# Two dense layers and the bus attention of the second level joined into one stage of a single-core network kernel

## The chip, the cores and the metric

The kernel runs on one core of one Trainium2 chip. It computes a whole four-level network in one launch. The metric is device time in microseconds (us), the median of the runs shown; lower is better. All arithmetic is in f32.

The engines are named as the profile names them: PE (TensorE, matrix multiplies, with PEld for its weight loads), DVE (VectorE), ACT (ScalarE), POOL (GpSimd) and SP (the queue that issues transfers). Each takes its own instructions in order; semaphores join them.

## The reference

The stream `x` has 4 batches of 512 tokens with 128 features (the reference sees the same numbers as 2 x 256 or 4 x 256 in other stages). Every block adds its result to `x` after a layer norm. The change touches three consecutive blocks of the second level:

```python
x = x + _L1_ffn_ref(_layernorm(x), W1, b1, W2, b2)
x = x + _L1_attn_b_ref(_layernorm(x), ...)
x = x + _L1_ffn_ref(_layernorm(x), W1, b1, W2, b2)
```

The dense block is two products with ternary weights and a rectifier between them:

```python
h = relu(einsum('bsd,fd->bsf', x, Wq1) + b1)      # 128 -> 512
out = einsum('bsf,df->bsd', h, Wq2) + b2          # 512 -> 128
```

The bus attention, cut to what matters:

```python
xn = _rms(x, w_norm_in)
route_in = xn.mean(axis=1)
probs = softmax(silu(route_in @ router_w1) @ router_w2 + router_b2)
ssm_out = scan(state = lam * state + (1 - lam) * xn)          # per channel, over tokens
a1, a2 = softmax(q1 k1 * sc), softmax(q2 k2 * sc)             # two heads of 32
slr_out = ((a1 - slr_lam * a2) @ v) @ slr_wo
mixed = ssm_out + (p_medium + p_full) * slr_out               # last token also gets arc_ctx
out = concat([mixed, xn]) @ mix_w
out = residual + _rms(out, w_norm_out)
summary = out.mean(axis=1) @ bus_compress
published = summary @ bus_publish
out = out + 0.1 * (published @ bus_expand)    # the softmax is over one key and is 1
```

## The kernel before

`x` stays on chip as `self.x`, 128 tokens on the partitions and 16 chunks of 128 features beside each other, four chunks to a batch. `moments` (lines 369 to 375) takes mean and variance of each chunk after every change of `x`, `normed` (377 to 393) makes the normalised copy `xn`, and `transposed` (360) turns four chunks into `xT`, with features on the partitions.

The program is a list of stages, `STAGES` (2881). One stage follows the other; the list has `"L1a", "L1f", "L1b", "L1f"`, so the dense layer `L1f` (1444) runs once before and once after the bus attention `L1b` (1486). Each stage opens its own pools for on-chip memory and for the eight banks of the matmul accumulator (PSUM), and closes them at its end.

`L1f` runs over the four batches. Per batch it multiplies four blocks of 128 x 128 by 512 columns (`ps_h`), ACT rectifies each (line 1459), 16 products of 128 x 128 x 128 sum into `ps_o` (1463), and DVE adds `ps_o` to `x` (`add_to_x`, 440) and takes moments. POOL adds the bias (`bias_x`, 434). Two banks hold `ps_h` and the transposes, two hold `ps_o`.

`L1b` is a pipeline of 16 scores, four per batch (`score`, 1578). A score is two products on 32 rows each into `ps_s` (two banks); DVE takes the row maxima (1586), ACT two exponentials with sums (1589), DVE the reciprocals (1593, 1594), POOL scales one half (1595), and DVE joins both into `a` (1598), which frees the banks. Three scores may be in flight (six banks); the last two banks serve everything else. `turn_scores` (1602) transposes `a` three slots later (`LAG`). A `Plan` (261) calls the other functions at slots written out by hand (1734 to 1751): the other batches' `turn`, `project` and `values`, the routers, and, for batch b, `context`, `mix` and `out` at slots 4b+7 to 4b+9. `finish` (1650) closes two batches at a time, batches 0 and 1 at slot 14, batches 2 and 3 after the loop: the root of the mean square on ACT (which needs another function table than the exponential), eight scalings on DVE, two additions per batch on POOL, and the mean over tokens on PE. Then two products by bus matrices are made for all four batches (1767), and each batch gets the result added and its moments taken (1772 to 1781).

The order of the work: everything called with `pin=True` or through `keep_in_program_order` stays in the order written; PE's matmuls in `L1b` are all pinned, as are the exponentials, and POOL's scalings there. Other DVE and ACT instructions are ordered by the framework's scheduler. At its start `L1b` calls `roots(0, B - 1)`, which waits for the moments of three batches, and then `turn(0)`. `net.there` (2905) tells the second `L1f` that only one batch is normalised at first. `L2a` (1784), the stage behind, calls `norm` (413), which normalises three batches unless the stage before it did so (`self.ahead`).

Of the kernel before, what the change touches and what calls it, by code (L numbers as in the profile page):

```python
# [11 lines left out]
F32 = mybir.dt.float32  # L12
# [262 lines left out]
class Net:  # L275
# [1168 lines left out]
    def L1f(self):  # L1444
        nc, tc = self.nc, self.tc
        w1, w2 = self.W("f1_w1"), self.W("f1_w2")
        with (
            tc.tile_pool(name="l1f_s", bufs=1) as sp,
            tc.tile_pool(name="l1f_r", bufs=2) as rp,
            tc.tile_pool(name="l1f_p", bufs=2, space=PSUM) as pp,  # L1450
        ):
            xT, rest = self.norm(pp, self.there)
            for b in range(B):
                self.bias_x(b, "f1_b2")
                h = rp.tile([P, 4, S], F32, name="h")
                for m in range(4):
                    ps = pp.tile([P, S], F32, tag="mm", name="ps_h")
                    self.mm(ps, w1[:, m * P : m * P + P], xT[:, b * S : b * S + S])
                    nc.scalar.activation(h[:, m], ps, AF.Relu, bias=self.W("f1_b1")[:, m : m + 1])
                po = pp.tile([P, CB, D], F32, tag="o", name="ps_o")  # L1460
                for j in range(CB):
                    for m in range(4):
                        self.mm(
                            po[:, j],
                            h[:, m, j * P : j * P + P],
                            w2[:, m * D : m * D + D],
                            start=m == 0,
                            stop=m == 3,
                        )
                self.add_to_x(b, po)  # L1470
                if b == 0:
                    rest()

# [12 lines left out]
    def L1b(self):  # L1486
# [5 lines left out]
        SC, EPS, LAG = 32.0**-0.5, 1.1920929e-07, 3  # L1492
        with (
            tc.tile_pool(name="l1b_s", bufs=1) as sp,
            tc.tile_pool(name="l1b_r", bufs=2) as rp,
            tc.tile_pool(name="l1b_p", bufs=1, space=PSUM) as pp,
        ):

            def bank(name, shape, tag="mm", bufs=2):
                return pp.tile(shape, F32, tag=tag, name=name, bufs=bufs)  # L1500

            mv = self.mv
            rs = sp.tile([P, 2, NC], F32, name="rs")
            tiny = sp.tile([P, 1], F32, name="tiny")
            nc.gpsimd.memset(tiny, EPS * 1e-5)
            x0 = sp.tile([P, NC, D], F32, name="x0")
            xh, xT = self.xn, self.xT

            def roots(b0, b1):
                cs = slice(CB * b0, CB * b1)
                var = mv[:, cs, 1]
                nc.scalar.activation(rs[:, 0, cs], var, AF.Sqrt, bias=tiny, scale=1.0 + EPS)
                nc.scalar.activation(rs[:, 1, cs], var, AF.Sqrt, bias=self.eps["1e-5"])
                nc.vector.reciprocal(rs[:, :, cs], rs[:, :, cs])


            def centred(out, b, k, eng):
                for c in range(CB * b, CB * b + CB):  # L1520
                    i = eng.tensor_scalar(
                        out[:, c],
                        self.x[:, c],
                        mv[:, c, 0:1],
                        rs[:, k, c : c + 1],
                        ALU.subtract,
                        ALU.mult,
                    )
                    if eng is nc.gpsimd:
                        tc.keep_in_program_order(i)  # L1530
# [3 lines left out]
            def turn(b):  # L1534
                centred(xh, b, 0, nc.vector)
                ps = bank("ps_tr", [P, CB, P])
                for j in range(CB):
                    self.tr(ps[:, j], xh[:, CB * b + j])
                i = nc.scalar.activation(
                    xT[:, b * S : b * S + S],  # L1540
                    ps.rearrange("p j t -> p (j t)"),
                    AF.Identity,
                    scale=self.W("b1_wni"),
                    accum_out=route[:, b : b + 1],
                )
                tc.keep_in_program_order(i)
# [4 lines left out]
            q, k, v, ema, a, aT, cT, mixed, y, t = ({} for _ in range(10))  # L1551

            def project(b):
                bs = slice(b * S, b * S + S)
                ps = bank("ps_q", [64, S])
# [3 lines left out]
                ps = bank("ps_k", [64, S])  # L1559
# [4 lines left out]
            def values(b):  # L1564
                ps = bank("ps_v", [P, CB, 32])
                for j in range(CB):
# [5 lines left out]
                i = nc.gpsimd.tensor_scalar(  # L1572
                    ema[b], xT[:, b * S : b * S + S], one_l, None, ALU.mult
                )
                tc.keep_in_program_order(i)
                nc.vector.tensor_tensor_scan(ema[b], lam, ema[b], 0.0, ALU.mult, ALU.add)

            def score(n):
                b, j = divmod(n, CB)
                ps = bank("ps_s", [P, 2, S], "sc", 3)  # L1580
                for h in range(2):
                    r = slice(32 * h, 32 * h + 32)
                    self.mm(ps[:, h], q[b][r, j * P : j * P + P], k[b][r, :], pin=True)
# [4 lines left out]
                for h, to in ((1, e), (0, ps[:, 0])):  # L1588
                    i = nc.scalar.activation(
                        to, ps[:, h], AF.Exp, bias=m[:, h : h + 1], accum_out=z[:, h : h + 1]  # L1590
# [1340 lines left out]
```

## Time and profile before

| what | value |
|---|---|
| median of 3 runs | 2410.75 us (2405.64 to 2413.52) |
| the profiled execution | 2416.43 us, span 2414.7 us |
| instructions | 33640 |
| PE busy in the span | 2156.9 us (89%), mean granted clock 0.928 |
| DVE, ACT, POOL busy | 1724.6 (71%), 1291.2 (53%), 610.4 us (25%) |
| first `L1f`: first transpose to last product | 1142.5 to 1176.0 us |
| `L1b`: to the first score, to the last score | 1184.6 us, 1270.1 us |
| second `L1f`: first `ps_h` to last product | 1310.7 to 1345.3 us |
| `L2a`: first product | 1354.4 us |

The span is what lies between the first and last instruction of the profiled execution; 1.7 us lie around it. All times inside it are counted from its start. "Granted clock" is the share of PE's full speed that the throttle let through in a window. A busy PE is not PE at its peak: at half clock the same product counts twice the busy time. The three stages that the change joins take 202.8 us here, 8.4% of the span.

### The profile page before, as it was taken

How to read it: one execution, taken by the hardware profiler on the slowest of the kernel's cores; microseconds unless marked ns; L12 is line 12 of the kernel's file. 1: busy time of each engine (PE TensorE's matmuls, PEld its weight loads, DVE VectorE, ACT ScalarE, POOL GpSimd, SP SyncE). 2: the span in 40 equal slices, each digit the busy share in tenths (PEclk: the TensorE clock that was granted, in tenths of full speed). 3: DMA queues.
4: the chain of work that ended last, by engine and by line, in shares of the span. 5: the costliest groups of instructions: out<-in, count | busy, mean ns of one | idle time of the engine just before them, and what ended most of it. 6: DMA issues, size and time to landing. Idle time of an engine off the chain costs nothing.

```text
span 2414.7 us, 33640 instructions
## 1 busy us (share of the span) xinstructions
PE 2156.9 (89%) x12151; PEld 1011.0 (42%) x12151; DVE 1724.6 (71%) x3373; ACT 1291.2 (53%) x2558; POOL 610.4 (25%) x441
## 2 busy tenths in 40 slices
PE   7999999999899998999876789889869998888868
PEld 2343334643333334667434446542214666422213
DVE  6666666579998774656464674679997557678995
ACT  4555555279845665342442463666645445476643
POOL 1100010010000001022153410048871015148871
PEclk9999999999899998999867989999989999988988
DMA  3000001400000000400200024245543430044550
GB/s 144 1 1 1 1 1 43 100 1 2 2 1 2 1 1 15 113 16 24 86 1 1 0 57 88 59 122 145 160 140 59 87 49 2 1 122 139 161 152 18
DMA packets 68885, 127.85 MB, mean 53 GB/s; under 512 B 9328, under 2 KB 29296, under 8 KB 68080
## 3 DMA queue, kind: packets, MB, share of 16 engines
q1 hardware_dynamic: 68720, 125.71, 19.8%
q8 instruction: 96, 1.57, 0.3%
q14 instruction: 69, 0.57, 0.1%
HBM read 119.91 MB, written 5.64 MB: 52 GB/s over the span
## 4 chain that ended last, share of the span: by engine, by line
PE 65%; DVE 16%; issue 9%; ACT 6%; DMA 2%; POOL 1%; SPq 0%; POOLq 0%; DVEq 0%; ACTq 0%
PE ps_o L346 14%; PE ps_s L346 9%; PE ps_st L346 6%; PE ps L346 5%; PE ps_c L346 5%; PE ps_g L346 4%; DVE hc L2373 4%; PE ps_x L346 3%; PE ps_u L346 2%; PE ps_v L346 2%; DVE ps_du L2368 2%; DVE e L850 2%; PE ps_tr L351 2%; PE ps_q L346 2%; DMA wt<-dram 2%
## 5 line engine op out<-in xcount | busy, mean ns | idle before, releaser
L2378 POOL TENSOR_TENSOR hc<-hc,cr 128x1024 f32<-128x1024 f32 x126 | 297.6, 2363 | 117.6 <-DVE hc L2373 112.8
L2373 DVE TENSOR_TENSOR_SCAN hc<-da,ps_du 128x1024 f32<-128x1024 f32 x128 | 291.0, 2275 | 0.0
L346 PE MATMUL ps_s<-k,q 32*128 32x512 f32 (+3 forms) x1088 | 254.1, 609 | 8.2 <-DVE mx L850 4.4
L538 ACT ACTIVATE e<-ps_s,mx 128x512 f32<-128x512 f32 x256 | 172.6, 686 | 139.5 <-DVE mx L533 132.9
L346 PE MATMUL ps_du<-du,spread 64*128 64x512 f32 x512 | 164.0, 713 | 64.6 <-DVE hc L2373 64.4
L2354 ACT ACTIVATE da<-da,am 128x512 f32<-128x512 f32 x248 | 165.8, 715 | 62.3 <-DMA da<-dram 57.5
L346 PE MATMUL ps<-xT,w_L2f 128*128 128x512 f32 (+1 forms) x416 | 194.6, 615 | 0.0
L936 DVE TENSOR_REDUCE nm<-ps_s 128x1 f32<-128x512 f32 x256 | 162.5, 683 | 37.7 <-PE ps_s L346 28.8
L1022 ACT ACTIVATE e<-ps_st 128x512 f32<-128x512 f32 x256 | 138.4, 595 | 88.7 <-PE ps_s L346 61.8
L533 DVE TENSOR_REDUCE mx<-ps_s 128x2 f32<-128x1024 f32 x128 | 150.9, 1219 | 43.8 <-PE ps_s L346 43.6
L2368 DVE TENSOR_TENSOR ps_du<-ps_du,br 128x1024 f32<-128x1024 f32 x128 | 154.9, 1211 | 30.3 <-PE ps_du L346 30.2
L861 ACT ACTIVATE e<-e,mx 128x512 f32<-128x512 f32 (+3 forms) x256 | 140.1, 549 | 18.7 <-DVE mx L850 18.4
L346 PE MATMUL ps_st<-q,k 32*128 32x512 f32 x512 | 143.6, 645 | 0.0
L346 PE MATMUL ps_s<-q,k 64*128 64x512 f32 x512 | 129.1, 618 | 2.2 <-ACT e L538 1.7
L346 PE MATMUL ps_c<-e,vz 128*64 128x512 f32 x512 | 123.5, 604 | 0.8 <-POOL vz L549 0.8
L1945 DVE SCALAR_TENSOR_TENSOR t<-ps,w_L2f,t 128x512 f32<-128x512 f32 (+1 forms) x104 | 76.7, 747 | 62.5 <-PE ps L346 41.7
L850 DVE CUSTOM_DVE_ANT_0 e<-ps_s,tri 128x512 f32<-128x512 f32 (+3 forms) x256 | 109.2, 485 | 14.7 <-PE ps_s L346 14.7
L346 PEld LDWEIGHTS ps_du<-du,spread 64*128 64x128 f32 x512 | 45.8, 203 | 173.3 <-issue 118.8
L346 PEld LDWEIGHTS ps_s<-k,q 32*128 32x128 f32 x1088 | 86.5, 196 | 72.8 <-issue 30.6
L346 PEld LDWEIGHTS ps<-xT,w_L2f 128*128 128x128 f32 (+1 forms) x416 | 75.7, 191 | 97.0 <-issue 75.2
L549 POOL TENSOR_TENSOR vz<-v,z 128x512 f32<-128x512 f32 x32 | 33.4, 1043 | 322.8 <-DVE z L547 293.7
L659 DVE TENSOR_TENSOR hc<-hc,wt 128x1024 f32<-128x1024 f32 x80 | 94.7, 1188 | 25.5 <-ACT hc L1948 12.2
(500 smaller groups left out, 4188.7 us busy)
## 6 DMA issues: line engine op xcount, KB each, us to landing
da<-dram SPq DMA_DIRECT2D x124, 256.0 KB
da<-dram SPq DMA_DIRECT2D x124, 255.5 KB
wt<-dram SPq DMA_DIRECT2D x144, 128.0 KB
wt<-dram SPq DMA_DIRECT2D x32, 256.0 KB
dram<-dl SPq DMA_DIRECT2D x16, 256.0 KB
wt<-dram SPq DMA_DIRECT2D x16, 224.0 KB
wt<-dram SPq DMA_DIRECT2D x16, 192.0 KB
wt<-dram SPq DMA_DIRECT2D x16, 160.0 KB
```

The costliest lines, as they stand in the source:

```text
L346: i = self.nc.tensor.matmul(out, lhsT, rhs, start=start, stop=stop)
L533: nc.vector.tensor_reduce(mx, sc, AX.X, ALU.max, negate=True)
L538: nc.scalar.activation(es[n][:, hh], sc[:, hh], AF.Exp, bias=mx[:, hh : hh + 1], accum_out=z[m][:, j, hh : hh + 1],)
L659: nc.vector.tensor_tensor(h, h, wt[b, k][:, r:e], ALU.mult)
L850: red = nc.vector.tensor_tensor_reduce(e[:, i, :w], sc[i][:, :w], tri[:, S - w :], -1.0, BIG, ALU.add, ALU.min, mx[:, i : i + 1],)
L861: nc.scalar.activation(e[:, i, :w], e[:, i, :w], AF.Exp, bias=mx[:, i : i + 1], scale=-1.0, accum_out=z[:, i : i + 1],)
L936: nc.vector.tensor_reduce(nm[:, j, i, 9:10], sc, AX.X, ALU.max, negate=True)
L1022: keep(nc.scalar.activation(es_[n][:, i], sc, AF.Exp))
L2354: nc.scalar.activation(da[n][:, t, t:], src[:, t:], AF.Exp, scale=am[:, at : at + 1])
L2368: keep(nc.vector.tensor_tensor(dx[n], dx[n], br, ALU.mult))
L2373: keep(nc.vector.tensor_tensor_scan(h, a, x, 0.0, ALU.mult, ALU.add))
L2378: keep(nc.gpsimd.tensor_tensor(hc[n], hc[n], cr, ALU.mult))
```

## The change

`L1f` and `L1b` go, and one stage `L1m` stands in their place; `STAGES` becomes `"L1a", "L1m", "L2a"`, and `net.there` goes. What differs inside:

- **One pipeline.** Batches 0 and 1 pass the first dense layer ahead of the loop, batches 2 and 3 in slots 0 to 7 beside the scores of batches 0 and 1. The second dense layer of batch b runs in slots 4b+12 to 4b+15; the loop has 28 slots, 16 of them with a score.
- **Per-batch finish.** `finish` is split into `out` (slot 4b+8), `weighed` (4b+9), `summary` (4b+10) and `normed` (4b+11), each for one batch.
- **Bus matrices multiplied once.** `transfer` (slot 5) makes the product of the three bus matrices by transposes, products and DVE copies. `summary` takes the token mean spread over 128 columns and needs one product per batch.
- **Roots on POOL.** Every inverse root in the stage is now two small POOL instructions, one that scales and adds, one that raises to the power -1/2. ACT's roots and DVE's reciprocals go.
- **Routers in pairs.** `router1` to `router3` and `marks1` to `marks3` run for two batches at a time, twice.
- **Banks.** Two scores in flight instead of three (four banks), three banks for everything else, one bank shared by `ps_o` and `ps_y`; `LAG` is 2 instead of 3.
- **Ahead of L2a.** `normed_ahead` in the last slot normalises batches 0 to 2 for `L2a`.

The core of the diff:

```diff
-    def L1f(self):
...
-    def L1b(self):
+    def L1m(self):
...
-        SC, EPS, LAG = 32.0**-0.5, 1.1920929e-07, 3
+        SC, EPS, LAG = 32.0**-0.5, 1.1920929e-07, 2
...
+            def root(out, in_, scale, eps):
+                keep(nc.gpsimd.tensor_scalar(out, in_, scale, eps, ALU.mult, ALU.add))
+                keep(
+                    nc.gpsimd.tensor_tensor(
+                        out, out, half.to_broadcast(list(out.shape)), ALU.pow
+                    )
+                )
...
+            def normed(b):
+                cs = slice(CB * b, CB * b + CB)
+                root(self.rs[:, cs], mv[:, cs, 1], 1.0, 1e-5)
+                self.centred(b)
+            def turned(b):
+                self.transposed(
+                    pp, "mm", xT[:, b * S : b * S + S], xn[:, CB * b : CB * b + CB], pin=True
+                )
+                self.bias_x(b, "f1_b2")
+                h[b] = rp.tile([P, 4, S], F32, name="h")
+            def hidden(b, m):
+                ps = bank("ps_h")
+                self.mm(ps, w1[:, m * P : m * P + P], xT[:, b * S : b * S + S], pin=True)
+                nc.scalar.activation(h[b][:, m], ps, AF.Relu, bias=self.W("f1_b1")[:, m : m + 1])
+            def dense(b, j):
+                if j == 0:
+                    po[b] = bank("ps_o", (P, CB, D), "o", 1)
+                for m in range(4):
+                    self.mm(
+                        po[b][:, j],
+                        h[b][:, m, j * P : j * P + P],
+                        w2[:, m * D : m * D + D],
+                        start=m == 0,
+                        stop=m == 3,
+                        pin=True,
+                    )
+                if j == CB - 1:
+                    self.add_to_x(b, po[b])
...
+            def residual(b):
+                cs = slice(CB * b, CB * b + CB)
+                root(rs[:, 1, cs], mv[:, cs, 1], 1.0, 1e-5)
+                scaled(x0, b, 1, nc.gpsimd)
...
-                ps = bank("ps_s", [P, 2, S], "sc", 3)
+                ps = bank("ps_s", (P, 2, S), "sc", 2)
...
-            def finish(b0):
...
+            def transfer():
+                w = self.W("b1_bc")
+                for n in ("b1_bp", "b1_be"):
+                    ps = bank("ps_t", (P, P))
+                    self.tr(ps, w)
+                    t = rp.tile([P, P], F32, name="busT")
+                    nc.vector.tensor_copy(t, ps)
+                    ps = bank("ps_w", (P, D))
+                    self.mm(ps, t, self.W(n), pin=True)
+                    w = bus if n == "b1_be" else rp.tile([P, D], F32, name="busw")
+                    nc.vector.tensor_copy(w, ps)
+            def summary(b):
+                ps = bank("ps_mean", (P, P))
+                for j in range(CB):
+                    self.mm(
+                        ps, y[b][:, j], self.ones, start=j == 0, stop=j == CB - 1, pin=True
+                    )
+                ctx = rp.tile([P, P], F32, name="ctx")
+                nc.vector.tensor_scalar(ctx, ps, 0.1 / S, None, ALU.mult)
+                ps = bank("ps_be", (P, D))
+                self.mm(ps, ctx, bus, pin=True)
+                xb = self.x[:, CB * b : CB * b + CB]
+                nc.vector.tensor_tensor(
+                    xb, ps.unsqueeze(1).to_broadcast([P, CB, D]), xb, ALU.add
+                )
+                self.moments(b)
...
+            def layer(b, n):
+                plan.at(n, turned, b)
+                plan.at(n, hidden, b, 0)
+                plan.at(n + 1, hidden, b, 1)
+                plan.at(n + 1, hidden, b, 2)
+                plan.at(n + 2, hidden, b, 3)
+                plan.at(n + 2, dense, b, 0)
+                plan.at(n + 2, dense, b, 1)
+                plan.at(n + 3, dense, b, 2)
+                plan.at(n + 3, dense, b, 3)
+            for b in (2, 3):
+                layer(b, 4 * b - 8)
+            for b in range(1, B):
+                if b > 1:
+                    plan.at(4 * b - 5, first_root, b)
+                plan.at(4 * b - 4, turn, b)
+                plan.at(4 * b - 2, project, b)
+                plan.at(4 * b - 1, values, b)
...
+            plan.at(5, transfer)
             for b in range(B):
...
+                n = 4 * b
+                plan.at(n + 2, residual, b)
+                plan.at(n + 6, context, b)
+                plan.at(n + 7, mix, b)
+                plan.at(n + 8, out, b)
+                plan.at(n + 9, weighed, b)
+                plan.at(n + 10, summary, b)
+                plan.at(n + 11, normed, b)
+                layer(b, n + 12)
+            self.ahead = False
+            self.normed(B - 1, B)
+            for b in range(2):
+                turned(b)
+                for m in range(4):
+                    hidden(b, m)
+            for j in range(CB):
+                dense(0, j)
+            first_root(0)
+            for j in range(CB):
+                dense(1, j)
+            first_root(1)
             turn(0)
...
+            last = 4 * B + 11
+            for n in range(last + 1):
                 if n < NC:
                     score(n)
...
+                if n == last:
+                    self.normed_ahead()
                 plan.run(n)
...
-    "L1a", "L1f", "L1b", "L1f",
+    "L1a", "L1m",
```

## The prediction

> **What bounds the kernel now.** First comes the page with its 40 slices of 60.4 us. The three stages lie at 1142 to 1345 us, slices 18 to 22, and there PE's busy share and PE's granted clock dip together:
>
> ```profile
> PE   7999999999899998999876789889869998888868
> PEclk9999999999899998999867989999989999988988
> ```
>
> Then the busy times by stretch, cut at the stages' borders. The columns are the stretch, its length, the busy time with the instruction count of PE, PEld, DVE, ACT and POOL, PE's clock, and the transfers:
>
> ```profile
> 1142.50:1176.00 33.50, 33.15 (x176) 22.91 (x176) 8.02 (x41) 13.57 (x22) 1.44 (x2) 0.95 0.48 194
> 1176.00:1184.60 8.60, 5.27 (x14) 1.76 (x14) 6.78 (x29) 2.51 (x8) 0.10 (x1) 0.80 0.00 0
> 1184.60:1258.00 73.40, 63.45 (x223) 27.94 (x223) 41.63 (x88) 35.36 (x88) 32.71 (x25) 0.65 0.00 1
> 1258.00:1270.10 12.10, 3.69 (x18) 3.58 (x18) 8.19 (x16) 5.35 (x9) 10.29 (x10) 0.67 0.00 0
> 1270.10:1310.70 40.60, 23.17 (x105) 14.78 (x104) 19.99 (x70) 9.32 (x19) 11.89 (x11) 0.67 0.00 1
> 1310.70:1345.30 34.60, 33.95 (x172) 22.51 (x172) 11.07 (x41) 12.92 (x21) 4.01 (x5) 0.91 0.00 1
> 1345.30:1354.40 9.10, 3.45 (x12) 2.22 (x13) 8.64 (x33) 4.17 (x6) 3.64 (x5) 0.62 0.00 0
> ```
>
> The two dense layers (first and sixth line) are bound by PE at nearly full clock. Between them PE has work for part of the time only, and does it at 0.65 to 0.67 of its speed. The fourth line is `finish(0)` in slot 14, the fifth holds the last score, `finish(2)`, the bus and the norm, the seventh opens L2a. Last, the chain of waits shows what the fifth line's end consists of:
>
> ```profile
> 1287.87 0.50 ACT y L1645
> 1288.39 1.28 ACT L357
> 1289.68 0.31 ACT ms L357
> 1290.02 0.21 DVE ms L358
> 1290.26 4.31 DVE y L1657 x8
> 1294.69 1.27 POOL y L1665
> 1296.01 1.88 PE ps_mean L346 x8
> ...
> 1310.10 0.59 ACT xT L365
> ```
>
> It is one serial walk through ACT, DVE, POOL and PE, in which PE is late with nothing. So the change can gain where PE idles or runs slowly, up to what the PE work itself takes.
>
> **The change, by four pieces.** The whole is 1142.5 to 1354.4, 211.9 us.
>
> *Front, now 33.5 + 8.6 = 42.1 us.* Ahead of the first score only two batches of dense work remain. In the steady run a batch took 7.2 us (its `ps_o` begins at 1157.4, 1164.6 and 1171.8). In the new order both batches' `ps_h` stand ahead of the first `ps_o`: transposes, copy and cold start 2.6, eight `ps_h` products of 0.93 (3.72 for four at 1323.1) with one copy of 0.6 between, 8.0, and `dense(0)` 3.6 end at 14.2. Adding to `x` and moments took 1.9 (1153.5 to 1155.5), a root I take as 0.8, one scaled chunk 0.34, and from the first transpose of `turn(0)` to the first score the trace has 6.3 (1178.3 to 1184.6). With 1.2 us for `dense(1)`'s addition on the same DVE, this is 25 us. `dense(1)` hides behind it. **Minus 17.**
>
> *Middle, first score to last score, now 73.4 + 12.1 = 85.5 us.* PE's work in slots 0 to 14, at full clock by rows at clock 1.00: 15 scores of 1.13 are 17; 13 transposes of scores of 0.66 are 8.6; three dense batches of 7.2 are 21.6 (none are in this stretch today); three projections of two products 5.6; values 3 x 1.0; contexts 3 x 1.06; `mix` 3 x 1.0; `out` 2 x 2.0; three turns 1.8; two summaries of five 128-column products 2.4; routers and `transfer` 2. Together 72 us. DVE, today 41.6 + 8.2, gains the dense additions and moments (7), the new norms and bus additions with moments (8), `transfer` and a second router set (4) and one more turn: 70 us. Neither fits much below 72, both lie on queues that wait for each other. Bounds: 72 if PE never waits, 144 if it runs at half clock throughout. I take a clock of 0.90 (the sixth line, dense work with a cold start, had 0.91; the third 0.65) and leave PE the 14% of idle time that the third line shows (10 of 73.4): 72 / 0.90 / 0.86 = 93 us. The fourth line's stall goes, since the finish is spread over three slots; DVE's eight scalings become four. **Plus 7.5.**
>
> The two score buffers are a wait added. From a score's first product to the end of its `a` (which frees the banks) 16 scores took 8.8 to 16 us, median 11.4. Behind the waiting score stand all pinned products, and ACT's and DVE's work on them. Two in flight allow a slot of 11.4 / 2 = 5.7 us, 86 us for 15, so 93 covers it. `transfer`'s four round trips over DVE stall PE some 4 us once and are in the 14%.
>
> *Tail, last score to last product, now 40.6 + 34.6 = 75.2 us.* PE's written order decides. The last score's own chain takes 9.2 (1270.1 to 1279.3), its transposes and copy 1.3; five pieces of dense work ahead of `context(3)` 4.6; `summary(2)` waits for POOL until 18; batch 2's `x` addition, moments, norm end at 25; `out(3)` stands behind `turned(2)` in slot 20 and ends at 29. Then batch 3's serial walk: copies 1.1, reduce 0.7, root 0.6, four scalings 2.2, POOL 1.3, mean 0.9, bus 0.7, addition 0.7, moments 1.6, root 0.6, norm 1.4, transposes and copy 1.2, handoffs 14 x 0.25: 16.5. Last a dense batch from a cold PE, as at 1310.7 to 1321.3: 10.6. Sum 56. The dense work of batches 1 and 2 is hidden in these waits. **Minus 19.**
>
> *L2a's opening, now 9.1 us.* Twelve normalised chunks (5 us of DVE) and one root with its table load (1.28) move under the last dense products. Left are transposes, a copy and the rest of the table loads: 4. **Minus 5.**
>
> Removed besides: four table loads of 1283 ns inside L1b, counted in the walks above. The transfers that SP issues at 1142.5 stay where they are.
>
> **Roots on POOL.** No row shows a power on POOL. Below, the smallest instruction there took 0.10 us (a memset of 128x1); above, the dearest plain one 2.35 (128x1024). I take the nearest in size, 0.29 for 128x32, so 0.6 for a root and 0.2 for its handoff. At 2.35, four roots on the path cost 16 more, and ten in the middle raise POOL's 53 us there to 100: together about +30.
>
> Sum: -17 + 7.5 - 19 - 5 = **-33.5 us**. The profiled execution's own time is 2416.4 (span 2414.7 and 1.7 around it), which gives 2383. It stands 5.7 above the median of the runs, so on the median I predict **2377**.
>
> **Two rules weighed.** The trace has PE idle for 2.38 us before 1239.24, and the clock goes from 1.00 to 0.54:
>
> ```profile
> 1236.00:1238.00 2.00, 0.87 (x6) 0.42 (x4) 0.74 (x2) 1.23 (x4) 1.10 (x1) 1.00 0.03 8
> 1238.00:1240.00 2.00, 0.76 (x1) 0.29 (x2) 1.46 (x4) 1.67 (x5) 0.78 (x2) 0.54 0.00 0
> ```
>
> The Trainium skill, "TensorE: Matmul & The Clock Gate", section "Why this matters for your kernels", lets PE idle up to some 3 us between bursts without a fall. By that rule the middle could keep clock 1.00, 72 / 0.86 = 84, and the time would be 2368; by the row short gaps cost clock too, which is why 0.90 stands above. The skill's "GPSIMD Engine Reference", section "Engine selection", speaks against the roots: elementwise work belongs on VectorE, GpSimd being about twice as slow. With twice my price the four roots on the path would add 2.4 us; no run here shows it yet.
>
> **Rivals.** *PE nearly full.* Half of the waits go, middle 78, time 2362 or less. For it: third line's clock was low because PE starved. Against: DVE at 70 of 78.
>
> *Small gain.* Either the power is dear (+30, 2407), or the two score buffers bind: with the longest latency, 16 us, a slot takes 8, the middle 120, and the time is 2404. For it: POOL's x0 (3.2 us) and the pinned additions stand before a score's scaling; DVE is busier, so latencies grow. Against: `finish` made the 16.
>
> *Slower.* The clock stays half in the pipeline: score products use 32 rows, and at 1188 to 1216 PE was mostly busy and yet at 0.50. Then the middle is 144, 51 more, and the time 2428. It decides below a mean clock of 72 / 126.5 = 0.57, with no wait at all. Against: dense products at 1162 to 1170 had 1.00, and from 1310.7 a busy PE got its clock back within 7 us, so half clock needs gaps that a PE with 144 us of work would not have.
>
> *It does not interleave.* PE's order is pinned as written, so the dense products do lie between the scores; only their readiness can fail, which is the small gain.
>
> **Chances.** Forecast (2362 to 2392) 0.60; PE nearly full (2345 to 2362) 0.15; small gain (2392 to 2418) 0.15, of which 0.06 within 0.3% (7.2 us, about what a measurement of this kernel can tell from no change); slower 0.10. So faster 0.60 + 0.15 + 0.09 = 0.84, same 0.06, slower 0.10. The range reaches half into PE nearly full and over the faster half of small gain: 2355 to 2405.
>
> **What would show it.** First score about 25 us after the first transpose; the last 93 us later; no gap like 1258 to 1265 on PE; clock 0.85 or more between them; last product 56 us after the last score, with PE waiting some 5 us twice; L2a's first product 4 us later; a root's two POOL instructions under 0.7 us. A mean slot over 7.5 us, a clock below 0.6, or roots over 2 us would make it wrong.

## The result and the profile after

The changed kernel takes 2414.02 us (median; 2407.70 to 2419.11), the kernel before 2408.80 us on the same chip (2402.14 to 2415.79). The ratio is 1.0019, with a 95% interval of 1.001 to 1.0027: slower by 2 to 7 us, which is within 0.3%. The prediction of 2377 us was wrong, and so was its range.

The profiled execution of the changed kernel has 2414.02 us, a span of 2412.3 us and 33685 instructions. The joined stage runs from 1137.0 us (first transpose) to 1350.7 us (first product of `L2a`). These are the 40 slices of the page, now of 60.3 us; the stage lies in slices 18 to 22:

```profile
PE   7999999999899998999778689888868998888868
PEclk9999999999899998998868989999989999988988
```

The dip is still there. The busy times by stretch, cut at the first score, the last score, the last dense product and `L2a`'s first product, show what became of each piece (columns as before: stretch, length, busy time and instruction count of PE, PEld, DVE, ACT and POOL, PE's clock, transfers):

```profile
1136.97:1158.00 21.03, 18.61 (x89) 12.47 (x90) 5.29 (x27) 6.74 (x11) 2.70 (x5) 0.84 0.76 308
1158.00:1165.00 7.00, 3.47 (x19) 1.76 (x17) 4.86 (x16) 2.65 (x4) 2.77 (x3) 0.93 0.00 1
1165.00:1285.40 120.40, 94.76 (x386) 51.83 (x386) 62.20 (x176) 47.13 (x113) 58.59 (x56) 0.74 0.00 1
1285.40:1343.70 58.30, 45.97 (x232) 31.02 (x228) 24.52 (x95) 18.04 (x31) 18.71 (x23) 0.87 0.00 1
1343.70:1350.70 7.00, 2.60 (x14) 2.15 (x13) 6.00 (x18) 1.17 (x2) 3.77 (x3) 0.84 0.00 0
```

| piece, us | before | predicted | after |
|---|---|---|---|
| front, to the first score | 42.1 | 25 | 28.0 |
| middle, first to last score | 85.5 | 93 | 120.4 |
| tail, to the last dense product | 75.2 | 56 | 58.3 |
| `L2a`'s opening | 9.1 | 4 | 7.0 |
| whole | 211.9 | 178 | 213.7 |

Three pieces came within 3 us of their terms. The middle is 27 us longer than forecast and eats all that the front and the tail gave. PE is idle in it for 120.4 - 94.76 = 25.6 us, against 18.4 before.

The stage is 1.8 us longer than in the profile of before, while the runs say 2 to 7. Each profile is of one execution, and what lies outside the stage varies too: the rest of the span is 2202.8 us in the profile of before, 2198.6 here, and 2194.7 to 2204.2 in the profiles of the experiments, which don't touch it. So below, an edit is judged by its stage as well as by its time.

PE's own lines, with the idle time before an instruction and what ended it in brackets, name the main waits of the middle:

```profile
1195.83 1.29 PE L351 MATMUL ps_tr<-ident,xn 128*128 128x128 f32 x4 [2.87 <-DVE rt_m L1451]
...
1231.71 1.16 PE L351 MATMUL ps_tr<-ident,xn 128*128 128x128 f32 x4 [5.86 <-DVE xn L1536]
...
1245.00 1.19 PE L346 MATMUL ps_mean<-ones,y 128*128 128x128 f32 x8 [2.78 <-POOL y L1686]
...
1263.52 1.25 PE L351 MATMUL ps_tr<-ident,xn 128*128 128x128 f32 x4 [3.99 <-DVE xn L393]
...
1283.09 0.49 PE L346 MATMUL ps_be<-bus,ctx 128*128 128x128 f32 x2 [2.19 <-DVE ctx L1712]
```

These five make 17.7 of the 25.6 us; the next is 2.37 us at 1170.48, for ACT's copy of batch 2's `xT`. No line waits for a score's banks. Each of the five waits for the end of a serial chain: a norm before its transposes, the finish before its mean, the mean before the bus product. (At 1195.83 the bracket names a router's instruction that DVE did between the norm's scalings. At 1283.09 the mean's `ctx` stood on DVE behind the joining of a score, which waited for POOL.) The longest, 5.86 us, belongs to `turn(3)` in slot 8, whose `first_root` was called in slot 7. POOL and DVE in those microseconds show the chain:

```profile
1227.10 0.17 DVE L375 BATCH_NORM_AGGREGATE ln_mv<-ln_st 128x2 f32<-128x6 f32 x1
...
1228.87 1.23 DVE L1598 TENSOR_TENSOR_SCAN ema<-w_L1b,ema 128x512 f32<-128x512 f32 x1 [0.49 <-POOL ema L1594]
...
1231.22 1.12 DVE L1536 TENSOR_SCALAR xn<-x,ln_mv,rs 128x128 f32<-128x128 f32 x4 [1.08 <-POOL rs L1483]
```

```profile
1227.28 1.56 POOL L1594 TENSOR_SCALAR ema<-xT,one_l 128x512 f32<-128x512 f32 x1 [1.87 <-DVE ln_mv L375]
1228.92 1.16 POOL L1481 TENSOR_SCALAR rs<-ln_mv 128x4 f32<-128x4 f32 x1
1230.16 1.02 POOL L1483 TENSOR_TENSOR rs<-rs,half 128x4 f32<-128x4 f32 x1
```

PE was done at 1225.85. The last moments end at 1227.27. Then POOL first does 1.56 us of another batch's scan input, which stands ahead of the root in its queue, then 2.2 us of root, and only then can DVE scale the first chunk. About 1 us of the root is no cost of its own: its first instruction took 1.16 us instead of the usual 0.19, and it ran beside DVE's scan (1228.87 to 1230.10) and ended with it.

### The profile page after: what moved, and what is told of

The parts are those of the page before. It is cut to its first block, busy times and chain, and to the rows that moved or that the text cites. A ratio compares the mean times of both kernels' runs of the same rounds, so it can differ in the third digit from the quotient of the medians.

```text
span 2412.3 us, 33685 instructions
## 1 busy us (share of the span) xinstructions
PE 2151.6 (89%) x12164; PEld 1013.3 (42%) x12164; DVE 1724.2 (71%) x3383; ACT 1283.5 (53%) x2551; POOL 631.6 (26%) x473
## 4 chain that ended last, share of the span: by engine, by line
PE 64%; DVE 16%; issue 8%; ACT 7%; DMA 2%; POOL 2%; SPq 1%; POOLq 0%; DVEq 0%; ACTq 0%
PE ps_o L346 13%; PE ps_s L346 9%; PE ps_st L346 6%; PE ps_c L346 5%; PE ps L346 5%; PE ps_g L346 4%; DVE hc L2436 3%; PE ps_x L346 3%; PE ps_u L346 2%; PE ps_du L346 2%; PE ps_v L346 2%; DVE e L850 2%; PE ps_y L346 2%; PE ps_tr L351 2%; DVE ps_du L2431 2%
## 5 line engine op out<-in xcount | busy, mean ns | idle before, releaser
L346 PE MATMUL ps_s<-k,q 32*128 32x512 f32 (+3 forms) x1088 | 250.2, 594 | 10.4 <-DVE mx L850 4.7
L533 DVE TENSOR_REDUCE mx<-ps_s 128x2 f32<-128x1024 f32 x128 | 150.9, 1219 | 43.8 <-PE ps_s L346 43.6
L351 PE MATMUL ps_tr<-ident,xn 128*128 128x128 f32 x256 | 52.6, 341 | 66.8 <-DVE xn L393 32.1
```

Of the source, the lines that this page charges most:

```text
L346: i = self.nc.tensor.matmul(out, lhsT, rhs, start=start, stop=stop)
L351: i = self.nc.tensor.transpose(out, in_, self.ident)
L533: nc.vector.tensor_reduce(mx, sc, AX.X, ALU.max, negate=True)
```

## The experiments

Four theories were set against each other. **Written order**: PE's order is pinned, and a chain called one slot ahead of its user leaves PE idle for what the chain lacks in distance. **Banks**: two scores in flight. **Roots**: the power on POOL. **Clock**: idle gaps and narrow products lower PE's clock, and that alone makes the length.

The table has every run. "Time" is the median, the ratio stands to the kernel before on the same chip with its 95% interval, and the last four columns come from the profile: the whole stage, its middle, PE's clock and PE's idle time (length less busy time) in the middle.

| run | time | ratio | stage | middle | clock | idle |
|---|---|---|---|---|---|---|
| changed kernel | 2414.0 | 1.0019 [1.001, 1.0027] | 213.7 | 120.4 | 0.74 | 25.6 |
| e1_cheap_root | 2405.8 | 0.9993 [0.9983, 1.0002] | 206.7 | 117.6 | 0.76 | 23.8 |
| e2_banks_free | 2412.9 | 1.0010 [0.9998, 1.0021] | 210.1 | 115.8 | 0.81 | 27.7 |
| e3_turn_later | 2413.1 | 1.0020 [1.0009, 1.003] | 213.3 | 118.6 | 0.76 | 26.1 |
| e4_finish_later | 2405.1 | 0.9992 [0.998, 1.0004] | 206.3 | 110.0 | 0.72 | 18.6 |
| e5_both_later | 2405.9 | 0.9992 [0.9978, 1.0005] | 204.5 | 112.3 | 0.78 | 25.8 |
| e6_not_interleaved | 2423.0 | 1.0062 [1.0039, 1.0086] | 225.5 | 98.6 | 0.71 | 31.7 |
| e7_filler | 2409.7 | 1.0012 [0.9998, 1.0026] | 209.9 | 119.8 | 0.83 | 15.2 |
| e8_all_later | 2398.2 | 0.9947 [0.9929, 0.9964] | 193.8 | 103.5 | 0.82 | 21.8 |
| e9_later_cheap_root | 2391.3 | 0.9935 [0.9918, 0.9952] | 189.3 | 100.3 | 0.85 | 21.8 |
| e10_later_two_banks | 2395.9 | 0.9957 [0.9942, 0.9973] | 197.4 | 104.2 | 0.77 | 19.4 |
| e11_transfer_early | 2403.5 | 0.9987 [0.9974, 0.9999] | 203.0 | 109.3 | 0.84 | 26.8 |
| e12_only_transfer | 2407.4 | 0.9997 [0.9983, 1.001] | 209.6 | 113.9 | 0.77 | 24.9 |
| e13_only_opening | 2409.9 | 1.0013 [0.9999, 1.0027] | 210.5 | 118.7 | 0.78 | 27.5 |

Below, an edit's worth is the difference of its ratio to 1.0019, times 2408.8. Two such intervals together leave each worth uncertain by some 3 to 4 us (up to 6 for e6 and e8 to e10, which have fewer runs). The middles are not all alike: where `summary` and the second dense layer come one slot later (e4, e5, e8 to e10), some work moves behind the last score. Busy time times clock, an estimate, gives 70 us of full-clock work in the changed kernel's middle, and 65 to 67 in these five. The whole stage is the fairer measure there.

**The price of the roots** (e1). The roots are not computed: a multiplication takes the power's place.

```diff
-                        out, out, half.to_broadcast(list(out.shape)), ALU.pow
+                        out, out, half.to_broadcast(list(out.shape)), ALU.mult
```

> The kernel after, with both instructions of each root kept, but the power replaced by a product with 1 and the first instruction giving 0.1 whatever its input: the norms are not computed, all else runs on its data as before. Three theories of why the stretch from the first to the last score took 120 us and not 93. Written order: PE must take its products in the order written, and in about every second slot it stands before one whose inputs come from a serial chain written only one slot earlier; the idle time also costs the clock. Banks: two scores in flight are too few. Roots: a power on POOL takes 1.03 us where I took 0.29. By roots, the stage gets shorter by 10 us or more, since POOL is free 0.8 us sooner in 16 places and the score's scaling waits behind it. By written order, 2 to 6 us, the part of seven waits that is the power itself. By banks, nothing beyond 2 us.

The groups of POOL show the price, first in the changed kernel (shapes, count, busy time and mean ns of one):

```profile
L1483 POOL TENSOR_TENSOR rs<-rs,half 128x4 f32<-128x4 f32 x6 | 6.2, 1032 | 0.5
```

and then in this run:

```profile
L1483 POOL TENSOR_TENSOR rs<-rs,half 128x4 f32<-128x4 f32 x6 | 1.2, 199 | 0.5
```

A power costs 1.03 us, 0.83 more than a multiplication of the same four columns. The wait of 5.86 us became 5.03, shorter by just this. Worth 6.3 us, the stage 7.0 shorter: between the two forecasts. More of it lies in front, tail and opening (4.2 by the stretches) than in the middle (2.8), so the price of the power is not what made the middle 27 us too long. The prediction's 0.6 us for a root was half of the 1.3 us that one took here in the usual case (0.19 and 1.03, with the gap between).

**Banks** (e2). The first half's exponential goes to SBUF, so that the banks come free before the join.

```diff
-                for i, to in ((1, e), (0, ps[:, 0])):
+                e0 = rp.tile([P, S], F32, name="e0", bufs=3)
+                for i, to in ((1, e), (0, e0)):
```

> The kernel after, with the second exponential written to a buffer on chip instead of back into the score's banks, so that the banks are free after ACT and not only after POOL and DVE, some 3 to 4 us sooner of the 7 to 13 us that they are held. By banks, the stretch between the scores falls from 120 us towards 93, by 15 us or more. By written order and by roots, it changes by less than 3 us.

Worth 2.2 us, not told from zero; the stage is 3.6 us shorter and the middle 4.6, where "banks" asked for 15 or more. PE's idle time stayed (27.7 us), though the clock rose. The banks are not the main cause.

**One slot more for the chains** (e3, e4, e5). In e3 `turn` and the routers come one slot later, in e4 `summary` and the second dense layer, in e5 both.

```diff
-                plan.at(4 * b - 4, turn, b)
+                plan.at(4 * b - 3, turn, b)
...
-                plan.at(n + 10, summary, b)
+                plan.at(n + 11, summary, b)
...
-                layer(b, n + 12)
+                layer(b, n + 13)
```

> The kernel after, with the transposes of batches 1 to 3 (turn) one slot later, behind the dense products of that slot, and the routers one slot later with them. By written order, the waits before these transposes (2.9 and 5.9 us for batches 2 and 3, and part of the 2.4 us around batch 1) shrink by half or more, and with the clock that they cost the stretch between the scores gets 6 to 15 us shorter. By banks and by roots, less than 3 us.

> The kernel after, with summary, the norm and the second dense layer of each batch one slot later (summary 4b+11, dense layer from 4b+13). By written order, the waits before the token means (2.8 us), the bus product (2.2) and the dense layers' transposes (4.0 and 3.5 us) shrink by half or more, and the stage gets 5 to 15 us shorter, the tail not longer. By banks and by roots, less than 3 us either way.

> The kernel after with both edits: turn and the routers one slot later, and summary, norm and second dense layer one slot later. Alone, the first changed the stage (first transpose of the dense layer to the first product of L2a) from 213.7 to 213.3 us and the second to 206.3. By written order, each alone leaves the other's waits standing, and together the stretch between the scores falls to 105 us or less and the stage to 200 or less. If turn's waits cost nothing of their own, the stage stays at 205 to 208.

"Written order" had forecast 6 to 15 us for e3 and a stage of 200 or less for e5, and missed both. e3 gained nothing: the 5.86 us wait is gone from PE's lines, and in its place stand new ones of 2.22 us (ahead of a score, for its banks), 2.53 and 2.93. e4 took the waits at 1245 and 1263 away and is worth 6.5 us (7.4 of the stage), as forecast, although its clock is lower. e5 is worth no more than e4. So distance helps where nothing else is late next, and that is only found out wait by wait.

**Without interleaving** (e6). The first dense layer of all batches stands ahead of the loop, the second behind it; all else is as changed.

```diff
-            for b in (2, 3):
-                layer(b, 4 * b - 8)
...
-                layer(b, n + 12)
+                layer(b, n + 24)
```

> The kernel after without the interleaving of the dense layers: all four batches of the first dense layer stand ahead of turn(0), all four of the second in slots 24 to 39. What stays is the finish by batch, the roots on POOL, the bus matrices multiplied once, the pairs of routers and two scores in flight. By written order, the front goes back to some 43 us, the stretch between the scores loses 21.6 us of dense work but keeps its waits, and takes 90 to 100 us, longer than the 85.5 of before; the tail is 65 to 75 us; the stage is 205 to 220. If the interleaving were the harm, the stage would be clearly below the 211.9 us of before.

This is 10.4 us slower than the changed kernel, so the interleaving is no loss. But it says what it is worth. The middle, now without any dense work:

```profile
1184.70:1283.30 98.60, 66.86 (x268) 32.98 (x268) 57.48 (x153) 38.48 (x98) 55.20 (x51) 0.71 0.00 1
```

It is 13.1 us longer than the 85.5 of the kernel before, which had no dense work there either. And the three dense batches, 21.6 us of PE at full clock, make it 120.4 - 98.6 = 21.8 us longer: as if no idle time had been there to take them in. PE's idle time fell only from 31.7 to 25.6.

Front (43.6) and middle came as forecast; the tail (76.1) and the stage (225.5) were longer than said.

**Clock** (e7). Extra full-width products, whose results are overwritten, stand ahead of the waiting transposes and means.

```diff
+            def filler(b, ps, n):
+                for _ in range(n):
+                    self.mm(ps, w1[:, 0:P], xT[:, b * S : b * S + S], pin=True)
...
+                if b > 0:
+                    filler(b, ps.rearrange("p j t -> p (j t)"), 3)
```

> The kernel after with useless full-size products put where PE waits: three of 128x128x512 ahead of the transposes of turn in batches 1 to 3, three ahead of those of the second dense layer, two ahead of each token mean, 29 in all, some 25 us of PE at full clock; their results are overwritten. A theory beside the waits: clock. In the trace after, PE fell to half clock in the waits and got it back only when full-width products came (1211.8, 1232.9, 1267.5), not through scores, transposes or contexts. By clock, the mean clock between the scores rises from 0.74 to 0.85 or more, and the stretch gets shorter although PE does more. If only the idle time counts, the stretch gets longer by 0 to 10 us, by what of the fillers stands beyond the waits.

```profile
1169.70:1289.50 119.80, 104.62 (x416) 54.59 (x416) 61.29 (x169) 46.96 (x113) 57.67 (x55) 0.83 0.00 1
```

PE's lines at the longest wait, and at the mean behind it:

```profile
1236.34 1.25 PE L351 MATMUL ps_tr<-ident,xn 128*128 128x128 f32 x4 [3.19 <-DVE xn L1542]
...
1249.76 1.16 PE L346 MATMUL ps_mean<-ones,y 128*128 128x128 f32 x8 [0.87 <-POOL y L1694]
```

The clock rose from 0.74 to 0.83, PE's idle time fell by 10 us, and the middle is as long as before, which neither theory had forecast. In full-clock terms (busy time times clock, an estimate) PE did 104.62 x 0.83 = 87 us of work against 94.76 x 0.74 = 70, so some 17 us of useless work fitted in. But it did not all fit into waits. In two places chains set the time, whatever PE does: the transposes of `turn(3)` start 66.7 us after the first score in both kernels, the mean 80.0 and 80.1 us after it, and both still wait behind their fillers. Elsewhere fillers stood where no wait was left: those at 1177.03 put the next score off by 3.1 us (11.5 us after the first score instead of 8.35), and quicker products won this back by the score in slot 6 (43.6 in both). So the equal length is partly a balance. The clock alone does not make the length, since both chains held their places at the higher clock; that PE's speed counts for nothing is not shown.

**All together** (e8). The edits of e2 and e5, and a third: the product of the bus matrices is made step by step between the dense products of the front, and batch 2's transposes and first hidden block stand ahead of the first score, `values(0)` behind it.

```diff
-            plan.at(5, transfer)
...
+            steps = transfer()
             for j in range(CB):
                 dense(0, j)
+                next(steps)
...
+            turned(2)
             project(0)
-            values(0)
+            hidden(2, 0)
```

> The kernel after with everything that the theories ask for: turn, routers, summary, norm and second dense layer one slot later; the second exponential written outside the score's banks; the product of the bus matrices made in the front, between the dense products; the transposes and the first product of batch 2 ahead of the first score, and the values of batch 0 behind it. By written order, the waits of 2.4 us at the first dense product, 2.6 at the first score and 4 for the bus matrices go as well: the front 25 us, the stretch between the scores 95 or less, the stage 190 or less, and the kernel faster than the one before by 0.5% or more.

This version is faster than both kernels: ratio 0.9947, 13 us below the kernel before (9 by the medians) and 17 below the changed one; its stage is 18.1 us shorter than the 211.9 of before. The 0.5% came as forecast, the stretches did not: 26.7, 103.5 and 193.8 us where 25, 95 and 190 were said.

Three runs then took it apart, and two more took its third edit apart.

> The version of e8 in which the roots are not computed: the power is a multiplication, the scale 0 and the added constant 0.1, on the same POOL instructions. In e1, against the changed kernel, this took 7 us from the stage. 'Written order' (a serial chain costs PE only what it lacks in distance from its use): in e8 the chains have one slot more, so the root's extra 0.9 us lies inside the slack, except on the serial walk at the end (three roots): minus 1 to 3 us against e8's 2398. 'Roots' (POOL itself is the bound, 60 us busy of 104 in e8's middle, wherever its users stand): the same 7 us again, 2391.

> The version of e8 with the banks of a score held until the joining of the halves, as in the changed kernel (the SBUF copy e0 is left out). 'Banks' (two scores in flight bind once the chains have more room): most of what e8 gained beyond e5 goes, 2404 to 2406, and PE waits ahead of ps_s. 'Written order': about what e2 showed alone, 1 to 4 us slower than e8, so 2399 to 2402.

> The changed kernel with only e8's third edit: the product of the bus matrices made step by step between the dense products of the front, the transposes and the first hidden block of batch 2 ahead of the first score, values(0) behind it. The changed kernel has waits of 2.4 us before 1170.5 (batch 2's xT) and some 3 us in slot 5 (transfer), both at half clock afterwards. 'Written order': these waits go, minus 6 to 9 us, 2405 to 2408. 'Banks' or 'roots': the middle stays at 120 and the time at 2412 to 2414.

In e9 the roots of e8 are not computed, as in e1: 0.0012 +- 0.0024 by the ratios, which decides nothing; by the profile the stage is 4.5 us shorter (193.8 to 189.3), between the two forecasts. Like e1, e9 computes no norms and is only a measurement. In e10 the banks are held again: the difference to e8 (0.0010, 2.4 us) is not told from zero either, but the stage is 3.6 us longer, as much as e2 had won. Its middle is as long as e8's (104.2 and 103.5 us) though its clock is 0.77 and not 0.82. e11 is the changed kernel with the third edit alone, and that edit is the largest single one: 7.7 us by the ratios, 11 us of the middle.

> The changed kernel with only the product of the bus matrices moved, out of slot 5 into the gaps between the dense products of the front. In the changed kernel its four round trips stand at 1204.1 to 1208.6, with PE at clock 0.50 from 1196 to 1215. 'Round trips' (a wait in a stretch at half clock also puts off the full-width products that bring the clock back): 4.5 us of the transfer and some 3 to 4 of the half clock behind it, so the middle is 112 to 113 and most of the 7.7 us of the last run is here, 2406 to 2408. 'Opening' (the half clock of 1165 to 1175 costs it): only the 4 us that were named in the prediction, 2410.

> The changed kernel with only batch 2's transposes and first hidden block put ahead of the first score and the values of batch 0 behind it. In the changed kernel PE waits 2.4 us for ACT's copy before 1170.5 and has clock 0.50 from 1165 to 1173. 'Round trips': 2 to 3 us, 2410 to 2412. 'Opening': 5 to 7 us, 2407.

e12 moves only the product of the bus matrices: worth 5.3 us, 6.5 us of the middle. e13 moves only batch 2's opening: 1.4 us, not told from zero. The changed kernel's PE in slot 5, where `ps_t` and `ps_w` are the bus matrices:

```profile
1204.11 0.58 PE L346 MATMUL ps_arc<-alT,w_L1b 64*128 64x2 f32 x2
1204.94 0.48 PE L351 MATMUL ps_t<-ident,w_L1b 128*128 128x128 f32 x1 [0.25 <-DVE arc L1782]
1205.90 0.77 PE L346 MATMUL ps_w<-w_L1b,busT 128*128 128x128 f32 x2 [0.48 <-DVE z L1616]
1207.05 0.47 PE L351 MATMUL ps_t<-ident,busw 128*128 128x128 f32 x1 [0.38 <-DVE busw L1702]
1207.91 0.80 PE L346 MATMUL ps_w<-w_L1b,busT 128*128 128x128 f32 x2 [0.38 <-DVE busT L1698]
1208.63 2.08 PE L346 MATMUL ps_s<-k,q 32*128 32x512 f32 x4
```

and the same place in e12:

```profile
1205.63 0.58 PE L346 MATMUL ps_arc<-alT,w_L1b 64*128 64x2 f32 x2
1206.14 1.19 PE L346 MATMUL ps_s<-k,q 32*128 32x512 f32 x4
```

From `ps_arc` to the score are 4.5 us in the one and 0.5 in the other. And the score behind takes 2.08 us in the one and 1.19 in the other: with the round trips there, PE stayed at half clock for another 6.6 us. Here PE's speed did count: 4.0 of the 6.5 us are the round trips, the rest nearly all slower products. It is no accident of one execution: in the seven profiles with the round trips ahead of this score (the changed kernel, e1, e2, e4, e6, e7, e13) it took 1.59 to 2.08 us, in the five with them in the front (e8 to e12) 1.13 to 1.19. By stretches, the changed kernel:

```profile
1204.00:1208.00 4.00, 2.50 (x8) 1.46 (x7) 1.17 (x6) 0.69 (x1) 0.77 (x1) 0.50 0.00 0
1208.00:1212.00 4.00, 4.00 (x11) 2.16 (x12) 2.17 (x3) 0.21 (x1) 0.79 (x1) 0.50 0.00 0
1212.00:1216.00 4.00, 4.00 (x18) 3.06 (x16) 0.33 (x2) 2.42 (x6) 0.58 (x1) 0.59 0.00 0
```

and e12 from its score on:

```profile
1206.00:1210.00 4.00, 3.45 (x17) 2.00 (x17) 2.27 (x5) 2.30 (x6) 1.57 (x1) 0.96 0.00 0
```

## Why the prediction was wrong, step by step

- **Front**: minus 14 where minus 17 was forecast. The order and the hiding of `dense(1)` were right. PE waited 2.60 us ahead of the first score for the copy of `k`, which DVE did behind a scan of 1.23 us; the root took 1.31 us, 1.45 with its handoffs, instead of 0.8.
- **Middle**: this is the step that failed. "I take a clock of 0.90" and "leave PE the 14% of idle time that the third line shows" became a clock of 0.74 and 21% (25.6 of 120.4). The 72 us of PE work were right: 94.76 x 0.74 is 70. With a clock of 0.74 and 14% the sum would be 72 / 0.74 / 0.86 = 113, the idle time does the rest. The 14% left out the stall of `finish(0)`, which was to go; over the whole middle of before the idle share was 21% (18.4 of 85.5), and so it stayed. But the form of the sum was wrong too. It let the added PE work fill PE's idle time, as if any ready product could. PE's order is fixed, so work fills only a wait that stands behind it in the written order, and the chains to the norm and the finish were called one slot ahead of their users. e6 shows it: the 21.6 us of dense work cost 21.8 us. The waits then cost clock as well, and at half clock the products that no chain held up took longer, as e12 shows behind the bus matrices. How the 27 us divide between waits and clock is not known, since no run changed the one without the other.
- **What the edits gave back, over the whole kernel**: the finish chain called too late 6.5 us (e4), the bus matrices in slot 5 5.3 (e12), the roots 6.3 over the whole stage (e1), the banks 2.2 and the opening 1.4 (both not told from zero), `turn` nothing alone. Their sum is 21.7 us; all at once, without the price of the power, gave 20.2 (e9), and 17.3 with it (e8). It is no single cause; with an uncertainty of 3 to 4 us on each piece, that the pieces add up is no more than fitting.
- **`transfer` "in the 14%"**: 4 us of round trips were forecast and seen, 4.5. What was not priced is the half clock that they prolonged.
- **Two banks**: the forecast was that a mean slot of 5.7 us would be allowed, so that they would not bind. In the changed kernel nothing waits for them ahead of a score: from a score's first product to the end of its `a` went 7.2 to 12.7 us, median 9.2, so two in flight would allow 4.6, and a slot takes 8.0 for other reasons. Right, though once `turn` is later a score does wait for them (2.22 us in e3). The prediction's own sign of failure, a mean slot over 7.5 us, did show.
- **Tail**: minus 17 where minus 19 was forecast. Batch 3's serial walk from ACT's copy at 1319.15 to its first `ps_h` at 1334.06 took 14.9 us, forecast 16.5. PE waited 3.47 us ahead of batch 1's transposes, and many times under 2.4, not "some 5 us twice".
- **`L2a`'s opening**: minus 2 where minus 5 was forecast. `normed_ahead`'s root is the one that stayed on ACT, and came only when the rectifiers were done: its table load ended at 1341.8. Twelve scalings then held DVE from 1342.42 to 1347.47, batch 3's addition stood behind them, and PE's first transposes behind that (the view begins at the second scaling):

```profile
1342.68 4.79 DVE L393 TENSOR_SCALAR xn<-x,ln_mv,ln_rs 128x128 f32<-128x128 f32 x11
...
1347.39 0.68 DVE L443 TENSOR_TENSOR x<-x,ps_o 128x512 f32<-128x512 f32 x1
...
1348.12 2.75 PE L351 MATMUL ps_tr<-ident,xn 128*128 128x128 f32 x12 [4.40 <-DVE x L443]
```

- **The rivals**: "small gain" named a middle of 120 us, and the middle is 120.4; but it put that down to banks or to a dear power, and the banks were not it, the power a part. So that number was luck. (The +30 for a dear power does not come out of its own terms either: they give 16 on the path, and 100 us of POOL against a middle of 93.) "Slower" by half clock did not come: the clock is well above 0.57. The kernel did become slower, by less than 0.3%, but not by that way. "PE nearly full" needs chains that are early; even e8 has 21.8 us of idle time.
- **What stays open**: e6's middle is 13 us longer than that of the kernel before with no dense work in it. It holds the roots, the finish per batch, the router pairs and the two banks; which of them makes the 13 us was not tried. Nor was it settled what keeps e8's middle at 103.5 us, 10 above the forecast with less work in it; its longest PE waits are 2.93 us for the routers' `dg` and 2.58 for a rectifier.

## What to carry to other kernels

In a pipeline whose matmul order is written by hand, work put in need not fill idle time: for each added piece, sum the serial chain that makes its input, with the queue that it stands in on each engine, and set that against the work written between the chain's start and its user. A factor for idle time or clock taken from part of the old stage did not carry over to the new one. One slot more helps only where nothing else is late next: it gave 6.5 us for the finish and nothing for `turn`. Once-only work with round trips is better placed where dense full-width products stand between its steps than in the loop; here that move alone gave back 5 us.

## What the runs showed of the hardware

- A power on POOL costs 1.03 us for 128x4 numbers, five times a multiplication (0.20). The Trainium skill, "GPSIMD Engine Reference", section "Engine selection", puts GpSimd at about half of VectorE's speed for elementwise work on two inputs; that does not foretell this price, since the multiplication on the same engine is cheap.
- The first, scaling instruction of a root takes 192 ns at best and 1161 at worst for the same 128x4 shape. The slow ones, at 1228.92 and 1260.82, ran beside DVE's scan of 1.23 us and ended with it. That they stood right behind other work on POOL is not it: the one at 1247.91 did so too and took 0.19. In the profiles of the changed kernel and of all experiments, the 29 that overlapped a scan took 1.16 to 1.17 us. The edit of e2 has a price of this kind: in e2, e8 and e9, 14 scalings beside DVE's joining, which there reads both halves from buffers, took 0.75 to 0.76 us. The other 181 took 0.19 to 0.20.
- PE's clock fell to half at waits of 2.87 us (before 1195.83 in the changed kernel) and 2.19 us (before 1283.09). The Trainium skill, "TensorE: Matmul & The Clock Gate", section "Why this matters for your kernels", allows gaps of some 3 us; here shorter ones sufficed, as the 2.38 us of the kernel before had. The length of the wait is not all that counts: the trace's clock records change only in steps of 3.41 us, and the first fall came at 1194.79, while PE was still waiting, at the end of a step in which it had been busy for 1.12 us. At what share the clock falls does not come out of these runs.
- It did not come back as soon as PE was busy. In the changed kernel scores on 32 rows, transposes, contexts, values and one full-width pair (`ps_slr`) filled these 8 us without a gap, at half clock throughout:

```profile
1248.00:1252.00 4.00, 4.00 (x16) 1.33 (x9) 3.14 (x11) 0.59 (x1) 3.81 (x6) 0.50 0.00 0
1252.00:1256.00 4.00, 4.00 (x16) 2.40 (x14) 1.15 (x5) 2.32 (x7) 0.46 (x1) 0.50 0.00 0
```

  The same section asks for 4 us of busy PE to get the full clock; these rows disagree. Full clock came at 1269.9, after 4 us of `ps_h` and `ps_y`, products of 128 rows and columns. In section "Part 4: PE-mode transpose" the page says that transposes do not count as busy in the same way; they are 1.1 of these 8 us, so they can be a part of it at most. Against the page stands the end of the stage: from 1348.39 to 1351.81 PE was busy throughout at half clock, 2.5 us of it with transposes, and had full clock from 1351.81. Which of the narrow products fails to count was not tried alone.
